# Bidirectional Mamba block with experts: both directions' outputs projected into one PSUM bank and added once a sequence

## The chip, the cores and the metric

The kernel runs on one core of a Trainium2 chip. It is one program whose five engines (TensorE, written PE in the profile; VectorE, DVE; ScalarE, ACT; GpSimd, POOL; SyncE, SP, which here only issues transfers) each work through a list of instructions in a fixed order and wait for one another by semaphores. The metric is the device time of one execution in microseconds (us), and less is better.

## The reference

The input x is 8 sequences of 512 tokens with 128 channels. It is normalised to xn, and the result is x plus an attention-like part of xn plus a mixture of experts of xn:

```
x   = x + attn(layernorm(x)) + ffn(layernorm(x))
attn: xn2 = layernorm(xn, g, b)
      out_f = mamba(xn2, f weights)
      out_b = reverse(mamba(reverse(xn2), b weights))
      attn  = concat(out_f, out_b) @ combine_w.T + combine_b + xn
mamba: xz = x @ in_w.T ; xi, z = split
      u = silu(conv4(xi)) ; dt, B, C = split(u @ x_w.T)
      delta = softplus(dt @ dt_w.T + dt_b)
      h[t] = h[t-1] * exp(delta*A) + delta*u * B[t]      (16 states)
      y = sum over states of h*C[t] + u*D ; return (y * silu(z)) @ out_w.T
ffn:  each token goes to the expert with the largest logit (8 experts):
      down(silu(gate(x)) * up(x))
```

A Mamba works on 256 inner channels with 16 states each. All numbers are float32. Both out_w and combine_w are linear, so the program multiplies them once at the start into one 256 x 128 matrix per direction, here called mo. The attention part of a sequence is therefore y_f times mo_f plus y_b times mo_b plus the bias combine_b.

## The kernel before

**Units and steps.** The work is cut into 16 units, one for each sequence and direction, in the order sequence 0 forward, sequence 0 backward, sequence 1 forward and so on. Units with an even number are forward passes, those with an odd number backward ones. A unit has 16 steps, one for each state, so the main loop of the program has 256 steps (and three more to empty the pipeline). In one step a state n of a unit is carried over all 512 tokens and both halves of 128 channels:

- `decay` (L764): ACT computes exp(delta*A) (L771) three steps ahead, and SP loads the row C of the state, spread over all partitions, from DRAM (`cs`, L778).
- `spread` (L792): PE brings delta\*u\*B into PSUM (tile `b`). For half of the states ACT has scaled it with B in `scaled` (L787), and PE only transposes it (L800). For the others PE spreads B over the partitions with a bfloat16 selector matrix (L805), and DVE multiplies it with delta\*u in `product` (L812).
- `scan` (L814): DVE runs the recurrence (L818), one instruction for each half.
- `times_c` (L835): POOL multiplies both halves of the state by C (L841). For a few states of the last unit C is brought into PSUM by a matmul in `spread_c` (L830) instead of by a transfer, and DVE multiplies (L839). [...]
- `sum_up` (L845): PE adds the product into the accumulator `py` in PSUM, three steps later (L855).

**What is woven in.** Everything else is put into the steps by hand. `plan` (L969) holds, for each step and each slot of a step ("ev", "ev2", "late", "pe0", "dv", "pe", "pe2"), what is to be issued there, and the loop at L1113 runs these slots in that order around the steps' own work. `prepare(v)` (L528) lists the preparation of unit v with its places in the steps of unit v-1: the norm, the input projection (`pi`), the convolution on DVE (L590), the gates (`pz`), the projection to dt, B and C (`px`), the step sizes (`pd`, L650), the softplus with a correction on POOL (`w`, L689 and L691 in `log1p` at step 9), and `delta` on DVE (L698) at steps 11 and 12, then delta times u on POOL (`du`, L709) and its transposes (`pdu`, L714). `conclude(v)` (L873) lists the end of unit v with its places in the steps of unit v+1: the gate (L881), the transposes back (`pyb`, L887 and L889) copied out by ACT (L906) at steps 4 and 5, the projection with mo (`po`, L914) in two halves at steps 7 and 8, and the addition to x by DVE (`total`, L929) at step 9. For a forward pass the bias is added to `po` by a float32 matmul of a row of ones with the bias (L921), one for each half of `po`. So an odd unit holds the projection of a forward pass, and an even one that of a backward pass. The last unit has an order of its own (`by_pairs`).

**The experts.** The tokens are ranked by expert in unit 1 and 2 (`arrange`). Then POOL scatters them with 32 indirect transfers to DRAM, sorted by expert (`scatter`, L408), one after the other from step 35 on, in units 2, 3 and 4 (L1007). From unit 4 on a group of four tiles of 128 sorted tokens is worked on in each unit: SP loads the tokens (`xe`, L434) and the weights (`we`, L422), PE runs the gate matmuls at steps 13 and 14 and the up matmuls of the group before in pieces at steps 3, 8 and 9 (`pg`, L457), DVE multiplies the two one step later each time (L481), and PE computes the way down at steps 10 and 11 (`pde`, L489). The results go back by indirect transfers (L500), are fetched at the end (`moe`) and added by POOL (L519).

**PSUM.** `py` has two of the eight banks, the tile `b` of `spread` rotates over four, and all other matmuls (`po`, `pg`, `pde`, `pd`, `pz`, `c` and so on) share two banks (`ps_mm`, L93). A matmul that takes one of these two waits until the tile that had it has been read.

```
ps_y, ps_b = pool("ps_y", 1, space=PS), pool("ps_b", 4, space=PS)
ps_mm = pool("ps_mm", 2, space=PS)
...
(7, "pe", do(project, range(2), False)),
(8, "pe", do(project, range(2, NJ), False)), (9, "dv", total),
...
for i in range(NT):
    add(o + 6 + i * 37 // NT, "ev", lambda i=i: scatter(i))
```

With o = 29 the last two lines put the scatters on the steps 35 to 70 without 42, 49, 57 and 64.

Of the kernel before, what the change touches and what calls it, by code (L numbers as in the profile page):

```python
# [32 lines left out]
F32 = mybir.dt.float32  # L33
BF16 = mybir.dt.bfloat16
# [5 lines left out]
P = 128  # L40
EPS = 1e-5
DIRS = ("f", "b")
L, D, DI, R, NS, KC, E = 512, 128, 256, 8, 16, 4, 8
NH, NJ = DI // P, L // P
# [6 lines left out]

ROWS, ROW_C, ROW_DT = 3 * NS, 64, 96
NX = ROW_DT + R


def columns():
# [20 lines left out]
def block_kernel(ctx: ExitStack, tc: tile.TileContext, a: dict, out: bass.AP):  # L77
    nc = tc.nc
    x = a["x"]
    NB = x.shape[0]  # L80
# [35 lines left out]

    rout = pk[:, at["rout"]]
    comb = halves("comb", D)
    comb_b = pk[0:1, at["comb_b"]]
    w = {}  # L120
    for i, d in enumerate(DIRS):
        w[d, "in"] = pk[:, at[d, "in"]]
# [65 lines left out]
    def selector():  # L188


        nothing = const.tile([P, 1], F32, name="nothing")
        nc.vector.memset(nothing, 0.0)
        for k in range(3):
            nc.gpsimd.affine_select(
                out=sel,
                in_=sel if k else nothing[:ROWS].unsqueeze(2).to_broadcast([ROWS, NS, P]), compare_op=ALU.not_equal, fill=1.0,
                base=-k * NS, pattern=[[-1, NS], [0, P]], channel_multiplier=1,
            )

    def project_weights(d, di):  # L200
        mo = const.tile([P, NH, D], F32, name=f"{d}_mo")
# [557 lines left out]
        return s % NS in sets.get(s // NS, BY_ACT)  # L759

    def c_in_psum(s):
        return s >= NSTEP - NS and s % NS in LAST_C

    def decay(s):  # L764

# [107 lines left out]
    def conclude(v):  # L873
# [20 lines left out]
        def block(y, h, j):  # L894
            return y[:, h, j, :] if len(y.shape) == 4 else y[:, h, j * P : (j + 1) * P]
# [6 lines left out]

        def back_end(h):
            if h == 0:
                c["y"] = tmp.tile([P, NH, L], F32, tag="y", name=f"y_{v}")
            nc.scalar.copy(c["y"][:, h, :], c["pyb", h])  # L906

        def project(js=range(NJ), whole=True):
            if whole or js[0] == 0:
                c["po"] = mm([P, NJ, D], f"po_{v}_{js[0]}")  # L910
            p = c["po"]
            for j in js:
                for h in range(NH):
                    nc.tensor.matmul(  # L914
                        p[:, j, :], block(c["y"], h, j), w[d, "mo"][:, h, :],
                        start=(h == 0 and (d == "b" or j == js[0])),
                        stop=(d == "b" and h == NH - 1), skip_group_check=(d == "f"),
                    )
            if d == "f":

                nc.tensor.matmul(  # L921
                    p[:, js[0] : js[-1] + 1, :], ones[0:1, :],
                    comb_b.unsqueeze(1).to_broadcast([1, len(js), D]),
                    start=False, stop=True, skip_group_check=True,
                )

        def total(js=range(NJ)):
            xs = xt[:, b * NJ + js[0] : b * NJ + js[-1] + 1, :]
# [1 line left out]

        def by_pairs():

            y = tmp.tile([P, NJ, NH, P], F32, tag="y", name=f"y_{v}")
            c["y"] = y.rearrange("p j h t -> p h j t")
            pairs = [range(k, k + 2) for k in range(0, NJ, 2)]
            for i, js in enumerate(pairs):
# [15 lines left out]
        if v == len(units) - 1:  # L952
# [3 lines left out]
            (2, "dv", gate),  # L956
            (3, "pe2", do(back, 0)), (4, "ev", do(back_end, 0)),
            (4, "pe2", do(back, 1)), (5, "ev", do(back_end, 1)),
            (7, "pe", do(project, range(2), False)),
            (8, "pe", do(project, range(2, NJ), False)), (9, "dv", total),  # L960
        ]

    def store(b):
        nc.sync.dma_start(
# [6 lines left out]
    def add(step, kind, f):  # L971
        plan[step, kind].append(f)
# [29 lines left out]
    for i, kind in (  # L1002
        (0, "dv"), (1, "ev"), (1, "dv"), (1, "pe2"), (2, "ev2"), (2, "dv"),
        (3, "dv"), (4, "ev"), (4, "dv"), (5, "ev"),
    ):
        add(o + i, kind, lambda: next(order_of, None))
    for i in range(NT):  # L1007
        add(o + 6 + i * 37 // NT, "ev", lambda i=i: scatter(i))

    begin = 4  # L1010
    groups = [list(range(k, min(k + GROUP, NK))) for k in range(0, NK, GROUP)]
# [37 lines left out]
        pass  # L1049
    weights("f")  # L1050
    selector()
    first.norm()
    first.turn()
    first.turn_end()
# [155 lines left out]
```

## Time and profile before

| | before |
|---|---|
| median of 3 runs | 952.93 us (952.07 to 959.26) |
| profiled execution | 953.34 us |
| its span, first to last instruction | 951.6 us |
| busy: PE, DVE, ACT, POOL | 850.2, 907.2, 803.0, 841.5 us |
| mean granted TensorE clock | 0.953 of full speed |
| `po` matmuls, forward and backward passes (L914) | 128 records each, 275 and 276 ns |
| bias matmuls (L921) | 32 records, 425 ns |
| additions to x (L929), 128 x 512 | 15, 677 ns |
| products with C on POOL (L841) and on DVE (L839) | 253 of 2362 ns; 6 of 679 ns |
| scatters (L409) | 32, 1015 ns |

The profile is one execution. A row of a group gives the line of the source, the engine, the operation, what it writes and reads with shapes, how often, and then the busy time in us with the mean of one in ns, and the idle time of the engine ahead of it with what ended it. A row of the timeline gives the start and the duration in us, the engine, the line and the operation, where neighbours of one kind are merged ("x8"), and in brackets the idle time ahead of it and what ended it. A float32 matmul is two records of the trace. Matmuls overlap one another, so a record's duration is longer than the distance to the next one.

### The profile page before, as it was taken

Reading aid. Unit: us, or ns where it says so; the run is one execution under the profiler, and the core shown is the slowest. Engines: PE = TensorE matmul, PEld = TensorE weight load, DVE = VectorE, ACT = ScalarE, POOL = GpSimd, SP = SyncE. Lnnn points to the kernel's source line nnn. Section 1 sums busy time; section 2 is a strip of 40 time slices with the busy share of each in tenths; the row PEclk is TensorE's granted clock in tenths of the full one; section 3 lists DMA queues with packets and bytes.
Section 4 is the critical chain, followed back from the end, with each engine's and each line's share of the span. In section 5 each row is a group of like instructions: output and inputs, shape, how many; then the busy total and the mean of one; then the engine's idle time right before and its main releaser. Section 6 shows DMA issues by size and latency. Waiting matters only on the chain.

```text
span 951.6 us, 16224 instructions
## 1 busy us (share of the span) xinstructions
PE 850.2 (89%) x5510; PEld 657.9 (69%) x5510; DVE 907.2 (95%) x1101; ACT 803.0 (84%) x1490; POOL 841.5 (88%) x524
## 2 busy tenths in 40 slices
PE   5699896978789889899998999989999999989897
PEld 2367574766567668777786877868777786767676
DVE  7999989999899999999999999999999999999996
ACT  5898986969679797998969989698988979799792
POOL 5689798799999979799897998979899898979995
PEclk9588999988979999999899999999999999999999
DMA  5364222222233625245441544425245341622262
GB/s 153 111 132 107 66 76 66 78 74 80 84 95 104 192 70 182 78 123 163 114 154 53 161 138 121 152 82 185 63 130 168 112 153 54 186 74 85 90 177 75
DMA packets 68483, 108.54 MB, mean 114 GB/s; under 512 B 6848, under 2 KB 29248, under 8 KB 68400
## 3 DMA queue, kind: packets, MB, share of 16 engines
q1 hardware_dynamic: 65552, 101.32, 36.0%
q0 software_dynamic: 2272, 4.67, 1.4%
q10 hardware_dynamic: 576, 1.51, 0.5%
q8 instruction: 44, 0.72, 0.3%
q14 instruction: 39, 0.32, 0.1%
HBM read 97.60 MB, written 9.87 MB: 113 GB/s over the span
## 4 chain that ended last, share of the span: by engine, by line
PE 42%; ACT 26%; DVE 18%; issue 7%; POOL 6%; DMA 1%; SPq 0%; POOLq 0%; DVEq 0%; ACTq 0%
PE py L855 14%; DVE hs L818 10%; ACT dA L771 8%; PE b L800 7%; ACT dbt L787 7%; PE pg L457 4%; PE pd L650 4%; POOL hs L841 3%; DVE b L812 3%; DVE acc L590 2%; PE pde L489 2%; PE po L914 2%; PE b L805 2%; ACT acc L582 1%; PE pdu L714 1%
## 5 line engine op out<-in xcount | busy, mean ns | idle before, releaser
L841 POOL TENSOR_TENSOR hs<-hs,cs 128x1024 f32<-128x1024 f32 x253 | 594.3, 2362 | 71.9 <-DVE hs L818 59.9
L818 DVE TENSOR_TENSOR_SCAN hs<-dA,b 128x512 f32<-128x512 f32 x512 | 592.8, 1206 | 0.1
L855 PE MATMUL py<-ident,hs 128*128 128x128 f32 x2048 | 279.3, 282 | 10.8 <-POOL hs L841 10.7
L855 PEld LDWEIGHTS py<-ident,hs 128*128 128x128 f32 x2048 | 234.4, 145 | 47.2 <-POOL hs L841 23.6
L787 ACT ACTIVATE dbt<-dut,bt 128x256 f32<-128x256 f32 x524 | 221.9, 496 | 0.1
L800 PE MATMUL b<-ident,dbt 128*128 128x128 f32 x1048 | 187.5, 289 | 19.6 <-DVE hs L818 10.4
L771 ACT ACTIVATE dA<-delta,b_A 128x512 f32<-128x512 f32 x256 | 168.2, 715 | 14.9 <-DVE hs L818 14.8
L800 PEld LDWEIGHTS b<-ident,dbt 128*128 128x128 f32 x1048 | 128.8, 145 | 74.1 <-ACT dbt L787 52.7
L771 ACT ACTIVATE dA<-delta,f_A 128x512 f32<-128x512 f32 x256 | 168.6, 715 | 8.3 <-DVE hs L818 6.3
L812 DVE TENSOR_TENSOR b<-du,b 128x512 f32<-128x512 f32 x250 | 159.8, 686 | 9.3 <-PE b L805 8.5
L599 PE MATMUL pz<-pk,xin 128*128 128x256 f32 x128 | 42.8, 492 | 29.3 <-DVE acc L590 25.4
L650 PE MATMUL pd<-cdt,pk 9*128 9x512 f32 x124 | 66.3, 635 | 0.0
L590 DVE SCALAR_TENSOR_TENSOR acc<-pi,pk,acc 128x511 f32<-128x511 f32 (+2 forms) x96 | 64.5, 739 | 0.1
L457 PE MATMUL pg<-xeT,we 128*128 128x128 f32 x468 | 61.8, 278 | 2.2 <-ACT z L610 2.1
L457 PEld LDWEIGHTS pg<-xeT,we 128*128 128x128 f32 x468 | 56.2, 192 | 5.5 <-ACT z L610 3.8
L599 PEld LDWEIGHTS pz<-pk,xin 128*128 128x128 f32 x128 | 30.2, 247 | 41.1 <-ACT dbt L787 26.5
L805 PE MATMUL b<-cdt,sel 48*128 48x512 bf16 x125 | 50.6, 405 | 8.6 <-DVE hs L818 8.6
L721 ACT COPY dut<-pdu 128x512 f32<-128x512 f32 x32 | 18.6, 585 | 34.6 <-PE pdu L714 34.6
L500 POOL DMA_INDIRECT by_token<-ye,to x39 | 39.6, 1016 | 6.3 <-issue 3.1
L646 POOL TENSOR_TENSOR cdt<-cdt 32x512 f32<-32x512 f32 (+1 forms) x32 | 33.1, 1034 | 7.8 <-ACT cdt L632 7.7
L489 PEld LDWEIGHTS pde<-we,g 128*128 128x128 f32 x234 | 27.6, 191 | 15.2 <-issue 7.6
L409 POOL DMA_INDIRECT sorted_in<-xn,row_i x32 | 32.5, 1015 | 5.3 <-issue 3.8
(170 smaller groups left out, 1054.8 us busy)
## 6 DMA issues: line engine op xcount, KB each, us to landing
cs<-cd SPq DMA_DIRECT2D x253, 256.0 KB, 3.5
we<-in_expert_w SPq DMA_DIRECT2D x39, 576.0 KB, 4.6
sorted_in<-empty SPq DMA_DIRECT2D x9, 258.0 KB, 7.9
xe<-sorted_in SPq DMA_DIRECT2D x9, 258.0 KB, 4.5
xt<-in_x SPq DMA_DIRECT2D x8, 256.0 KB, 7.3
moe<-by_token SPq DMA_DIRECT2D x8, 256.0 KB, 3.0
out<-xt SPq DMA_DIRECT2D x7, 256.0 KB, 3.7
pk<-in_pack ACTq DMA_DIRECT2D x1, 704.0 KB, 7.9
```

The costliest lines, as they stand in the source:

```text
L457: nc.tensor.matmul(p[:, q - 4 * b, :], T[ks[i]][:, which, c, :], G[ks[0], "xT"][:, i, :], start=True, stop=True,)
L590: nc.vector.scalar_tensor_tensor(c["acc"][:, h, k:], c["pi", h][:, : L - k], cw[:, h, KC - 1 - k : KC - k], c["acc"][:, h, k:], ALU.mult, ...
L599: nc.tensor.matmul(p[:, j, :], c["xin"][:, t : t + P], w[d, "in"][:, DI:], start=True, stop=True,)
L650: nc.tensor.matmul(p, w[d, "dt"][:, h * P : (h + 1) * P], cdt[ROW_DT : NX + 1], start=True, stop=True,)
L771: nc.scalar.activation(k["dA"][:, h, :], c["delta"][:, h, :], AF.Exp, scale=w[d, "A"][:, h, n : n + 1],)
L787: nc.scalar.activation(k["dbt"][:, j, :], c["dut"][:, j, :], AF.Copy, scale=c["bt"][:, j, n : n + 1],)
L800: nc.tensor.transpose(k["b", h][:, j * P : (j + 1) * P], k["dbt"][:, j, h * P : (h + 1) * P], ident,)
L805: nc.tensor.matmul(k["b", 0], sel[:, n, :], c["bc"], start=True, stop=True)
L812: nc.vector.tensor_mul(k["b", h], c["du"][:, h, :], k["b", 0])
L818: nc.vector.tensor_tensor_scan(k["hs"][:, h, :], k["dA"][:, h, :], k["b", h], 0.0, ALU.mult, ALU.add)
L841: nc.gpsimd.tensor_mul(k["hs"], k["hs"], k["cs"].unsqueeze(1).to_broadcast([P, NH, L]))
L855: nc.tensor.matmul(c["py"][:, j, h * P : (h + 1) * P], block[:, h, j * P : (j + 1) * P], weight, skip_group_check=True, **kw,)
```

## The change

There are three edits and a new timetable.

1. For sequences 0 to 6 the forward pass is no longer projected by itself. Its y is kept (the tile moves from a pool of one buffer to one of two), and when the backward pass of the sequence is concluded, PE projects both into one `po`: for each of the four token blocks two matmuls with mo_f and two with mo_b, at steps 7 and 8 as before. DVE adds the sum to x once. `total` moves from step 9 to step 10, for all units that have it. Sequence 7 keeps its two projections.
2. The bias is brought into `po` first, by one bfloat16 matmul over all 512 columns with a contraction of three rows. Three rows of the packed weights hold the bias, and `bias_pieces` (two subtractions on POOL at the start) leaves in them three pieces whose bfloat16 upper halves add up to the float32 value. The stationary operand is three rows of ones in bfloat16.
3. For state 6 of unit 3, C comes by a matmul into PSUM, and DVE multiplies, as for three states of the last unit; the load of C and the product on POOL go.
4. The scatters are put on the steps 35 to 71 without 40, 48, 52, 55 and 66.

In the order of the built program nothing else moves: ACT's list is the same, POOL's has the three new instructions at the start, one product less, and some scatters before or behind other neighbours.

```diff
--- before.py
+++ after.py
@@ -51,6 +51,9 @@
 
 ROWS, ROW_C, ROW_DT = 3 * NS, 64, 96
 NX = ROW_DT + R
+
+
+SCATTER, SCATTER_C = 3, (6,)
 
 
 def columns():
@@ -116,7 +119,10 @@
 
     rout = pk[:, at["rout"]]
     comb = halves("comb", D)
-    comb_b = pk[0:1, at["comb_b"]]
+    comb_b = pk[0:3, at["comb_b"]]
+    bias = comb_b.bitcast(BF16).rearrange("p (n two) -> p n two", two=2)[:, :, 1]
+    one_row = const.tile([3, P], BF16, name="one_row")
+    nc.gpsimd.memset(one_row, 1.0)
     w = {}
     for i, d in enumerate(DIRS):
         w[d, "in"] = pk[:, at[d, "in"]]
@@ -196,6 +202,12 @@
                 in_=sel if k else nothing[:ROWS].unsqueeze(2).to_broadcast([ROWS, NS, P]), compare_op=ALU.not_equal, fill=1.0,
                 base=-k * NS, pattern=[[-1, NS], [0, P]], channel_multiplier=1,
             )
+
+    def bias_pieces():
+
+
+        for m in (2, 1):
+            nc.gpsimd.tensor_sub(comb_b[:m], comb_b[:m], bias[:m])
 
     def project_weights(d, di):
         mo = const.tile([P, NH, D], F32, name=f"{d}_mo")
@@ -759,7 +771,7 @@
         return s % NS in sets.get(s // NS, BY_ACT)
 
     def c_in_psum(s):
-        return s >= NSTEP - NS and s % NS in LAST_C
+        return s % NS in {SCATTER: SCATTER_C, len(units) - 1: LAST_C}.get(s // NS, ())
 
     def decay(s):
 
@@ -902,27 +914,33 @@
 
         def back_end(h):
             if h == 0:
-                c["y"] = tmp.tile([P, NH, L], F32, tag="y", name=f"y_{v}")
+                c["y"] = two.tile([P, NH, L], F32, tag="y", name=f"y_{v}")
             nc.scalar.copy(c["y"][:, h, :], c["pyb", h])
 
         def project(js=range(NJ), whole=True):
-            if whole or js[0] == 0:
+
+            both_dirs = b < NB - 1
+            new = whole or js[0] == 0
+            if new:
                 c["po"] = mm([P, NJ, D], f"po_{v}_{js[0]}")
             p = c["po"]
+            biased = both_dirs or d == "f"
+            if new and biased:
+
+                nc.tensor.matmul(
+                    p, one_row, bias.unsqueeze(1).to_broadcast([3, NJ, D]),
+                    start=True, stop=False, skip_group_check=True,
+                )
+            terms = [(c["y"], w[d, "mo"])]
+            if both_dirs:
+                terms.insert(0, (C[v - 1]["y"], w["f", "mo"]))
+            terms = [(y, m, h) for y, m in terms for h in range(NH)]
             for j in js:
-                for h in range(NH):
+                for i, (y, m, h) in enumerate(terms):
                     nc.tensor.matmul(
-                        p[:, j, :], block(c["y"], h, j), w[d, "mo"][:, h, :],
-                        start=(h == 0 and (d == "b" or j == js[0])),
-                        stop=(d == "b" and h == NH - 1), skip_group_check=(d == "f"),
+                        p[:, j, :], block(y, h, j), m[:, h, :], start=not biased and i == 0,
+                        stop=i == len(terms) - 1, skip_group_check=biased,
                     )
-            if d == "f":
-
-                nc.tensor.matmul(
-                    p[:, js[0] : js[-1] + 1, :], ones[0:1, :],
-                    comb_b.unsqueeze(1).to_broadcast([1, len(js), D]),
-                    start=False, stop=True, skip_group_check=True,
-                )
 
         def total(js=range(NJ)):
             xs = xt[:, b * NJ + js[0] : b * NJ + js[-1] + 1, :]
@@ -930,7 +948,7 @@
 
         def by_pairs():
 
-            y = tmp.tile([P, NJ, NH, P], F32, tag="y", name=f"y_{v}")
+            y = two.tile([P, NJ, NH, P], F32, tag="y", name=f"y_{v}")
             c["y"] = y.rearrange("p j h t -> p h j t")
             pairs = [range(k, k + 2) for k in range(0, NJ, 2)]
             for i, js in enumerate(pairs):
@@ -956,9 +974,10 @@
             (2, "dv", gate),
             (3, "pe2", do(back, 0)), (4, "ev", do(back_end, 0)),
             (4, "pe2", do(back, 1)), (5, "ev", do(back_end, 1)),
+        ] + ([] if d == "f" and b < NB - 1 else [
             (7, "pe", do(project, range(2), False)),
-            (8, "pe", do(project, range(2, NJ), False)), (9, "dv", total),
-        ]
+            (8, "pe", do(project, range(2, NJ), False)), (10, "dv", total),
+        ])
 
     def store(b):
         nc.sync.dma_start(
@@ -1004,8 +1023,10 @@
         (3, "dv"), (4, "ev"), (4, "dv"), (5, "ev"),
     ):
         add(o + i, kind, lambda: next(order_of, None))
+
+    dates = [s for s in range(o + 6, o + 6 + 37) if s not in (40, 48, 52, 55, 66)]
     for i in range(NT):
-        add(o + 6 + i * 37 // NT, "ev", lambda i=i: scatter(i))
+        add(dates[i], "ev", lambda i=i: scatter(i))
 
     begin = 4
     groups = [list(range(k, min(k + GROUP, NK))) for k in range(0, NK, GROUP)]
@@ -1049,6 +1070,7 @@
         pass
     weights("f")
     selector()
+    bias_pieces()
     first.norm()
     first.turn()
     first.turn_end()
@@ -1178,7 +1200,7 @@
         c = slice(at["dt"].start + i * DI, at["dt"].start + (i + 1) * DI)
         pack[ROW_DT:NX, c] = v["dt_w"].T
         pack[NX, c] = v["dt_b"]
-    pack[0, at["comb_b"]] = inputs[pre + "combine_b"]
+    pack[:3, at["comb_b"]] = inputs[pre + "combine_b"]
     src["pack"] = pack
 
 
```

## The prediction

> **What bounds it.** I read the page's engine rows first, then the groups, then the waits of DVE and POOL, then the timeline of the stretches that the change touches.
>
> ```profile
> PE 850.2 (89%) x5510; PEld 657.9 (69%) x5510; DVE 907.2 (95%) x1101; ACT 803.0 (84%) x1490; POOL 841.5 (88%) x524
> ...
> L841 POOL TENSOR_TENSOR hs<-hs,cs 128x1024 f32<-128x1024 f32 x253 | 594.3, 2362 | 71.9 <-DVE hs L818 59.9
> L818 DVE TENSOR_TENSOR_SCAN hs<-dA,b 128x512 f32<-128x512 f32 x512 | 592.8, 1206 | 0.1
> ```
>
> DVE is idle for only 44 of 951.6 us: over the span it is the bound. But four engines are above 80%, so the question at each place is who is late there. DVE's own waits answer it:
>
> ```profile
> 196.97 0.70 DVE L698 SCALAR_TENSOR_TENSOR pd<-pd,w 128x512 f32<-128x512 f32 x1 [1.85 <-POOL w L691]
> 257.56 0.70 DVE L698 SCALAR_TENSOR_TENSOR pd<-pd,w 128x512 f32<-128x512 f32 x1 [4.02 <-POOL w L689]
> ...
> 439.29 1.29 DVE L812 TENSOR_TENSOR b<-du,b 128x512 f32<-128x512 f32 x2 [0.93 <-PE b L805]
> 475.54 1.29 DVE L812 TENSOR_TENSOR b<-du,b 128x512 f32<-128x512 f32 x2 [0.39 <-PE b L805]
> 478.31 0.69 DVE L929 TENSOR_TENSOR xt<-po,xt 128x512 f32<-128x512 f32 x1 [0.35 <-PE po L921]
> 479.40 0.69 DVE L481 TENSOR_TENSOR g<-g,pg 128x512 f32<-128x512 f32 x1 [0.40 <-PE pg L457]
> ```
>
> The reader is to see two regimes. In the scatter stretch (171 to 314 us) DVE waits for POOL, which the timeline shows with no wait for data from 171 to 329. Elsewhere DVE waits a few tenths for PE, above all in steps 7 to 9 of a unit, where po is computed. POOL waits for DVE early in every later unit (for 3.66 us at 855.64, the last time); after that it runs without a data wait to its last product at 941, so what DVE loses or gains after 856 doesn't reach the end.
>
> **The steps.** An odd unit carries the projection of a forward pass, an even one that of a backward pass. Costs below are distances from one start to the next in the timeline: scan 1.13, a 128x512 add 0.58, a half po (8 records) 0.9 to 1.0.
>
> (1) Odd units (1, 3, ... 13) lose po and the add. PE: 2 x (1.0 + 0.65 for the float32 bias of 256 columns) = 3.3 to 3.5 us less. DVE: the 0.58 add goes, and with it waits on a late PE. Unit 1: 0.58 + 0.35 (po) + 0.33 (b) + 1.06 (pd) = 2.3, taken as 2.0, since ranking the tokens follows. Unit 5: 0.58 + 0.17 = 0.75. Unit 7: 0.58 + 0.39 + 0.35 + 0.40 + 0.24 = 1.96. Units 9, 11, 13: 0.58 + 0.38 + 0.24 = 1.2 each. What is late next: at step 12 PE transposes du, which POOL writes (L709, ended 493.66 in unit 7). From there 0.5 for pdu, 1.0 for pg and 0.33 + 0.43 for b lie ahead of the product of state 16, which started at 497.11: no earlier than 495.9, a gain of 1.2. So unit 7 is capped at 1.2. Sum without unit 3: 2.0 + 0.75 + 4 x 1.2 = **-7.6**.
>
> (2) The scatter stretch. Of state 6 in unit 3 POOL loses its 2.36 us product; DVE gets two of L839 (679 ns, 1.2 to 1.4 us). Two scatters, 1.18 apart with their gap, move from before step 57 to after it, one from before step 41. At 257.56 POOL is then 2.36 + 2 x 1.18 = 4.7 us earlier and DVE's 4.02 wait nearly gone. But the scatters come back: by step 75 (313.96, where DVE waits 0.18 for POOL again) POOL has saved only the product. So the stretch, unit 3's add with it, gains **-2.4** and not 4.7. Ends: 0 (the product's slot filled by some other wait) and 4.7. The new matmul c (three took 3.4 us, 1.13 each) lies in a unit where PE is 82% busy; it holds a PSUM bank until DVE is through, and pd of step 6 may wait for it: 0 to 0.6, taken as 0. SP loses one 256 KB load. The last scatter goes from step 70 to 71, and SP's load of xe (306.14) waits for it; xe is read at 321.1, and the cs loads behind it in SP's queue have buffers of six: hidden, about 2 us if not.
>
> Here a rule speaks against the change. The Trainium skill (Perfetto Trace Analysis, Optimizing Scalar/DVE Operations) says that GpSimd and DVE share an SBUF port which a two-port DVE operation locks, so that moving work between them might not help. By it the stretch would gain nothing and pay 1.3. The row: L841 took 2338 to 2392 ns in a stretch where DVE worked beside it all the time, so POOL isn't being held up, and the product is worth its whole 2.36. I go with the row.
>
> (3) Even units. The doubled po costs PE 0.33 (bf16 bias, priced by L805, the same 512 columns) + 1.0 at step 7 and 0.9 at step 8: +2.3. Behind it stand b of the next states and the expert's pg, and DVE waits for those. The slack, in unit 10:
>
> ```profile
> 643.52 1.06 PE L914 MATMUL po<-b_mo,y 128*128 128x128 f32 x8
> 643.71 1.21 DVE L678 SCALAR_TENSOR_TENSOR w<-q,one 128x1024 f32<-128x1024 f32 x1
> 644.51 0.40 PE L805 MATMUL b<-cdt,sel 48*128 48x512 bf16 x1
> 645.95 1.28 DVE L812 TENSOR_TENSOR b<-du,b 128x512 f32<-128x512 f32 x2
> 645.99 1.06 PE L914 MATMUL po<-b_mo,y 128*128 128x128 f32 x8
> 646.88 1.06 PE L457 MATMUL pg<-xeT,we 128*128 128x128 f32 x8
> ...
> 648.26 0.67 DVE L929 TENSOR_TENSOR xt<-po,xt 128x512 f32<-128x512 f32 x1
> 648.84 0.69 DVE L481 TENSOR_TENSOR g<-g,pg 128x512 f32<-128x512 f32 x1
> ```
>
> b starts at 645.73 instead of 644.51, is done 0.43 later, and L812 is late by 0.21. po's second half runs 647.21 to 649.01, then pg to 650.11. The add is now a step later, so L481 is next in DVE at 648.47: it waits 1.64. Together 1.85 us; replayed to step 14 (b at 662.0 for 660.3) it stays 1.8. The add's later place costs nothing itself: the next pg waits for L481, not for the add. Part comes back: at state 16 DVE waits 0.93 for a b held up by POOL's du (the row at 439.29; 0.92 and 0.87 in units 10 and 12). So 1.8 - 0.9 = 0.9 in units 6, 10, 12. In unit 8 PE is already 0.91 late, so 0.21 becomes 0.73, and nothing comes back: 2.4. In unit 14 about 1.5, hidden behind POOL. Units 2 and 4 have no pg there and run in POOL's stretch: 0. Sum 3 x 0.9 + 2.4 = **+5.1**, between 1 (all absorbed) and 9 (nothing back, unit 14 visible).
>
> Another rule weighs against (1) and (3): the Trainium skill (TensorE: Matmul & The Clock Gate, What's actually happening) says PE falls to half clock after an idle window of about 3.4 us. Thinned odd units could then run a window of PE's steps at half speed, 1.7 us each, +10 over six units. The row: from 616 to 632 PE was busy 6.6 and 5.9 of each 8 us and the granted clock stayed 1.00; an odd unit without po is thinned no further than that. By the row 0.
>
> (4) Nothing: the bias pieces (two POOL subtractions, each under L646's 1.03) and the memset lie in POOL's 7.68 us wait before L646 at 22.08; uncovered about 2 us. y in two buffers frees no recorded wait. In the last unit the bias saves PE 0.9 and moves the add; POOL's chain sets that end: 0.
>
> **Sum:** -7.6 - 2.4 + 5.1 = -4.9. The profiled execution took 953.34 (span 951.6), 0.4 above the median of the runs shown; from the median 952.93 the same -4.9 gives **948.0**.
>
> **Rivals.** *Better than summed* (0.20): the cap on unit 7 doesn't hold, the stretch keeps 4.7, the 0.46 waits at state 18 of units 7 to 13 go, and the even units absorb their delay but for unit 8's 0.9: -2.3 - 4.7 - 0.75 - 2.4 - 3 x 1.66 + 0.9 = -14.2, 939. For it: PE runs without a gap through these steps, so 3.4 us is much relief. Against: POOL's du chain. *Only the instructions go* (0.16): waits are replaced by others; six adds of 0.58 and the POOL product save 5.9 and the even units take 5.1: 952. This is also the case that the change doesn't do what it says: the adds go but DVE idles in their place. *The doubled po becomes PE's bound* (0.14), which ends slower: with a half clock window in steps 7 to 9 of the even units (0.57 was granted from 528 to 532), the added 2.3 becomes 4.6 and DVE loses 1.8 + 2.3 = 4.1 in each of units 6, 8, 10, 12, of which 0.9 comes back in three: 16.4 - 2.7 - 10.0 = +3.7, 956.6. It decides from 2.5 us net lost per unit on (10.0 / 4). Against: the clock was 1.00 there in three of these four units.
>
> **Numbers.** Forecast 0.50, 948.0. A measurement of this kernel can tell about 1% from no change: below 943.4 or above 962.5. Faster by over 1% is most of the first rival and a tail of the forecast, 0.20; slower by over 1% is the part of the last rival where it goes further than worked out, 0.06; the rest 0.74. The range 939 to 957 holds the forecast's bounds, the second rival, and half of the other two.
>
> **To see after.** Right: no L929 in odd units, eight 128x512 adds in all for fifteen; the wait at the first delta of unit 3's step 11 gone or under 1 us, a new one of about 2 us for POOL's w at step 11 of unit 4; DVE waiting 1 to 2 us for pg in units 6 to 14. Wrong: pg waits of 3 us and more, a clock below 0.9 in steps 7 to 9 of even units, or no POOL wait left in unit 4 (the stretch gained more).

## The result and the profile after

The changed kernel took 956.62 us in the median of 20 runs (953.88 to 965.48), the kernel before, timed beside it, 952.9: ratio 1.0043 with a 95% interval of 1.0028 to 1.0059, that is +4.1 us (2.7 to 5.6). The forecast was 948.0, so the time went the other way. Executions over 1.5% above the fastest of the same kernel are left out of every median, ratio and mean clock below. The profiled execution of the changed kernel took 959.61 (span 957.9, granted clock 0.938), 3 us above its median; what is read from it below is read unit by unit and held against other executions.

The page's engine row and first groups, then four rows of the groups by form (busy us, mean ns, idle time ahead):

```profile
PE 857.1 (89%) x5488; PEld 666.0 (70%) x5488; DVE 903.8 (94%) x1096; ACT 804.0 (84%) x1490; POOL 840.7 (88%) x526
...
L853 POOL TENSOR_TENSOR hs<-hs,cs 128x1024 f32<-128x1024 f32 x252 | 592.4, 2363 | 79.3 <-DVE hs L830 56.8
L830 DVE TENSOR_TENSOR_SCAN hs<-dA,b 128x512 f32<-128x512 f32 x512 | 592.3, 1204 | 0.1
```

```profile
L940 PE MATMUL po<-f_mo,y 128*128 128x128 f32 x128 | 20.0, 281 | 0.0
L947 DVE TENSOR_TENSOR xt<-po,xt 128x512 f32<-128x512 f32 x8 | 5.3, 666 | 0.0
L851 DVE TENSOR_TENSOR hs<-hs,c 128x512 f32<-128x512 f32 x8 | 5.1, 680 | 4.3 <-PE c L842 4.3
L930 PE MATMUL po<-pk,one_row 3*128 3x512 bf16 x8 | 3.2, 398 | 0.0
```

The change did what it says: eight 128x512 adds for fifteen, one POOL product less, and a bias matmul of 0.40 us a record, like the matmul of L805 that it was priced by. DVE is busy 3.4 us less and yet ends later, so it waits more.

### The profile page after: what moved, and what is told of

Same layout as the page of the kernel before. It is cut to its first block, busy times and chain, and to the rows that moved or that the text cites. A ratio compares the mean times of both kernels' runs of the same rounds, so it can differ in the third digit from the quotient of the medians.

```text
span 957.9 us, 16171 instructions
## 1 busy us (share of the span) xinstructions
PE 857.1 (89%) x5488; PEld 666.0 (70%) x5488; DVE 903.8 (94%) x1096; ACT 804.0 (84%) x1490; POOL 840.7 (88%) x526
## 3 DMA queue, kind: packets, MB, share of 16 engines
q10 hardware_dynamic: 576, 1.51, 0.5%
## 4 chain that ended last, share of the span: by engine, by line
PE 46%; ACT 28%; DVE 15%; issue 5%; POOL 4%; DMA 1%; SPq 0%; POOLq 0%; ACTq 0%; DVEq 0%
PE py L867 15%; ACT dA L783 10%; ACT dbt L799 7%; DVE hs L830 7%; PE b L812 7%; PE pg L469 4%; PE pd L662 4%; PE pde L501 3%; DVE b L824 3%; POOL hs L853 2%; DVE acc L602 2%; PE po L940 2%; PE b L817 2%; PE pz L611 2%; PE pyb L901 1%
## 5 line engine op out<-in xcount | busy, mean ns | idle before, releaser
L867 PE MATMUL py<-ident,hs 128*128 128x128 f32 x2048 | 285.3, 286 | 11.9 <-POOL hs L853 11.7
L867 PEld LDWEIGHTS py<-ident,hs 128*128 128x128 f32 x2048 | 240.0, 147 | 45.1 <-issue 22.2
L812 PE MATMUL b<-ident,dbt 128*128 128x128 f32 x1048 | 190.0, 294 | 25.0 <-DVE hs L830 13.6
L812 PEld LDWEIGHTS b<-ident,dbt 128*128 128x128 f32 x1048 | 132.7, 149 | 78.4 <-ACT dbt L799 55.5
L611 PE MATMUL pz<-pk,xin 128*128 128x256 f32 x128 | 45.3, 515 | 28.3 <-DVE acc L602 24.8
```

The source lines that it names most:

```text
L611: nc.tensor.matmul(p[:, j, :], c["xin"][:, t : t + P], w[d, "in"][:, DI:], start=True, stop=True,)
L812: nc.tensor.transpose(k["b", h][:, j * P : (j + 1) * P], k["dbt"][:, j, h * P : (h + 1) * P], ident,)
L867: nc.tensor.matmul(c["py"][:, j, h * P : (h + 1) * P], block[:, h, j * P : (j + 1) * P], weight, skip_group_check=True, **kw,)
```

## Where the time went, unit by unit

A unit's length here is the distance from its first scan to the next unit's in the timeline. Setting all profiles side by side, the lengths of units 6 to 13 are not scattered: they take a few values, set by whether po is there and by whether a window of half clock (a stretch in which the granted clock is 0.50) lies on steps 7 to 8.5. There stand po, `one` (a matmul of one column, from which DVE forms w) and w. In each of the 19 traces the granted clock is either 1.00 or 0.50 and only changes at places a multiple of 3.41 us apart.

| unit | no half clock at steps 7 to 8.5 | half clock there |
|---|---|---|
| odd, forward po as before | 56.26, 56.25 (units 9 and 11 before) | 57.83 (unit 7 before) |
| odd, no po | 56.18, 56.16 (units 9 and 11 after) | 56.19, 56.14 (units 7 and 13 after) |
| even, po of one direction | 56.65 (unit 10 before) | 56.93 (unit 8 before) |
| even, doubled po | 57.71 (unit 8 after) | 59.28 (units 6, 10 and 12 after) |

So without a half clock window an odd unit gains 0.1, where 1.2 was predicted, and an even one pays 1.05, where 0.9 was predicted; with a window the odd one gains 1.6 and the even one pays 2.3. (Two windows in a row, at steps 7 to 9 of unit 13 of e3 below, made an odd unit without po 57.66 long.) A pair loses about 1.0 in the first case and 0.7 in the second. Unit 14 is hidden, as predicted: what it loses (1.15) unit 15 gives back. That holds without a window; with one on unit 14 (e16 below: 58.45) units 14 and 15 took 1.6 more than before. Unit 10 of the changed kernel (start, duration, engine, line; in brackets the idle time ahead and what ended it):

```profile
640.39 2.22 PE L662 MATMUL pd<-cdt,pk 9*128 9x512 f32 x4
...
643.46 1.91 PE L867 MATMUL py<-ident,hs 128*128 128x128 f32 x8
645.30 0.42 PE L697 MATMUL one<-ones 1*128 1x1 f32 x2
645.83 1.22 DVE L690 SCALAR_TENSOR_TENSOR w<-q,one 128x1024 f32<-128x1024 f32 x1 [1.00 <-PE one L697]
...
648.88 1.09 PE L867 MATMUL py<-ident,hs 128*128 128x128 f32 x8
648.99 1.30 DVE L824 TENSOR_TENSOR b<-du,b 128x512 f32<-128x512 f32 x2 [0.80 <-PE b L817]
...
652.91 0.69 DVE L493 TENSOR_TENSOR g<-g,pg 128x512 f32<-128x512 f32 x1 [1.51 <-PE pg L469]
```

The 1.51 for pg is the wait that was predicted (1.64). The eight py records at 643.46 take 1.91, those at 648.88 take 1.09: PE was at half clock ahead of po, `one` came 1.00 late and b 0.80. Of the scatter stretch, the first and last row are all of the waits for POOL that are left, and the two between are the longest of the others:

```profile
197.12 0.70 DVE L710 SCALAR_TENSOR_TENSOR pd<-pd,w 128x512 f32<-128x512 f32 x1 [0.25 <-POOL w L703]
...
225.07 1.29 DVE L893 TENSOR_TENSOR yt<-py,z 128x512 f32<-128x512 f32 x2 [1.59 <-PE py L867]
239.00 1.28 DVE L851 TENSOR_TENSOR hs<-hs,c 128x512 f32<-128x512 f32 x2 [1.35 <-PE c L842]
...
313.09 0.70 DVE L710 SCALAR_TENSOR_TENSOR pd<-pd,w 128x512 f32<-128x512 f32 x1 [0.46 <-POOL w L701]
```

The 4.02 at 257.56 are gone. In exchange DVE waits 1.35 for the new c, which the prediction left out, and 1.59 for py, where it waited 0.55 before.

## The experiments

The theory after the result: the scatter edits gain what was said, the odd units' relief is worth nothing, and the even units pay for the doubled po. The rival: windows of half clock make the loss, wherever po is.

| kernel | median us | ratio to before, 95% | mean clock of its runs |
|---|---|---|---|
| after | 956.62 | 1.0043 (1.0028 to 1.0059) | 0.949 |
| e1_scatter_only | 950.33 | 0.9967 (0.9952 to 0.9982) | 0.956 |
| e2_joint_only | 960.03 | 1.0055 (1.0031 to 1.0079) | 0.942 |
| e3_no_fwd_half | 949.94 | 0.9974 (0.9955 to 0.9994) | 0.944 |
| e4_po_behind_pg | 955.00 | 1.0005 (0.9987 to 1.0024) | 0.954 |
| e5_pd_128_rows | 955.38 | 1.0020 (0.9993 to 1.0047) | 0.954 |
| e6_du_first | 955.02 | 1.0003 (0.9980 to 1.0026) | 0.946 |
| e7_po_unread | 955.88 | 1.0018 (1.0004 to 1.0033) | 0.952 |
| e8_scatter_du_first | 949.25 | 0.9938 (0.9914 to 0.9962) | 0.956 |
| e9_pd_128_du_first | 952.90 | 1.0001 (0.9982 to 1.0020) | 0.952 |
| e10_best | 946.70 | 0.9933 (0.9913 to 0.9954) | 0.963 |
| e11_no_fwd_po | 947.92 | 0.9945 (0.9925 to 0.9966) | 0.950 |
| e12_split_late | 957.87 | 1.0066 (1.0041 to 1.0091) | 0.949 |
| e13_seq0_apart | 961.08 | 1.0086 (1.0055 to 1.0116) | 0.942 |
| e14_seq3to6_joint | 958.13 | 1.0047 (1.0028 to 1.0066) | 0.943 |
| e15_scatter_again | 950.30 | 0.9966 (0.9950 to 0.9981) | 0.955 |
| e16_after_again | 956.61 | 1.0047 (1.0025 to 1.0069) | 0.946 |
| e17_before_again | 954.05 | 1.0005 (0.9989 to 1.0021) | 0.953 |

Each ratio is to executions of the kernel before that were timed side by side with it; these had a mean clock of 0.950 to 0.952. The kernels were timed in groups: after; e1 to e4; e5 to e8; e9 to e12; e13 to e15; e16 and e17. Differences between kernels of different groups carry some 2 us of uncertainty, an estimate from the widths of the intervals. Within the changed kernel's 20 runs, 0.01 of mean clock goes with 3.3 us of time (correlation -0.75).

### The parts: e1, e15, e2, e3

e1 and e15 are the kernel before with `SCATTER, SCATTER_C`, `c_in_psum` and `dates` of the diff; e2 is the changed kernel without them. e3 leaves the forward terms out of the joint po:

```diff
-            if both_dirs:
-                terms.insert(0, (C[v - 1]["y"], w["f", "mo"]))
```

> The kernel before with only the C of state 6 of unit 3 by PSUM and the new scatter dates. Theory (the scatter stretch gains as summed, the loss lies in the even units): about 950.9, that is -2.0 against before, with DVE's waits for POOL between 171 and 314 us down from 5.9 to about 1 us. Rival (the stretch's waits are only replaced by others): within 0.5 of before, 952.9. Rival (POOL and DVE hamper each other): slower than before by up to 1.3.

> The changed kernel with C of state 6 of unit 3 and the scatter dates as before, so only the joint projection, the bias in pieces and the add at step 10. Theory (the joint projection is the whole loss, the stretch pays back 2): about 958.6, that is +5.7 against before. The steps as predicted would give -2.5 (950.4). If the stretch's edits were the loss: about 952.

> The changed kernel leaving out the forward half of the joint projection (16 of the 32 records of po in each even unit; the outputs lack that part), so that an even unit's PE has the work it had before plus the bf16 bias, and an odd unit none. Theory (the doubled po in the even units is the loss, odd units give nothing): the pg waits of 1.5 us in units 6 to 14 shrink to about 0.4, and the time falls by 4 times 1.9 to about 949. By the prediction's sum it would fall to 943 (the -7.6 of the odd units would then stand alone). Rival (half clock windows, whatever the length of po, make the loss): stays within 1 of 956.6, with granted clocks below 0.92 again in steps 5 to 7 of the even units.

> The kernel before with the C of state 6 of unit 3 by PSUM and the new scatter dates once more, as the base of the other two: about 950.3, 0.997 of the kernel before.

The scatter edits gain 3.1 and, again, 3.2 us: the step was right and a little small. The joint projection alone costs 5.2. e3 splits it: against e1 it only has the relief of the odd units (with the bias pieces, y's second buffer and the add's later place), and it is not faster, 0.9974 against 0.9967. Its runs had a mean clock of 0.944 for 0.956, so half clock has a part in this; but in its profile unit 11 takes 56.16, 0.1 less than in e1, and with windows units 7, 9 and 13 take 56.81, 56.88 and 57.66. Putting the forward half back (after against e3) costs 0.0069, 6.6 us. The odd units' -7.6 are therefore the step that is missing, and the even units' +5.1 came out at 6.6.

### po behind pg: e4

```diff
-            (8, "pe", do(project, range(2, NJ), False)), (10, "dv", total),
+            (8, "pe3", do(project, range(2, NJ), False)), (10, "dv", total),
```

with a slot "pe3" run after "pe2".

> The changed kernel with the second half of po issued behind the expert's up matmuls (pg) of step 8 instead of ahead of them. Theory (DVE's wait for pg is most of the loss of an even unit): the waits of 1.5 us for pg go in units 6 to 14, up to 1.5 in each of units 6, 8, 10 and 12, part of which comes back as a wait for b or for the next pg one step later: 951 to 954. Rival (half clock windows ahead of po make the loss): the pg waits go, but the time stays within 1 of 956.6.

The wait for pg at step 8's end goes, and comes back a step later as 0.97 for the next pg, and as 0.24 for pd (unit 10, at 650.54 and 657.72). Units 6, 10 and 12 take 57.70, 57.70 and 57.71, what a doubled po takes without a half clock window in the other order. It is PE's amount of work between steps 7 and 10 that costs 1.05, not its order. This profile has one half clock window at steps 7 to 8.5 (unit 8) for five in the changed kernel's. The kernel gains 1.6 by the medians and 3.6 by the ratios, where 2.6 to 5.6 were expected; the mean clock of 0.954 for 0.949 would make 1.7 of that, an estimate at the 3.3 us for 0.01 above.

### POOL's chain: e6 and e8

```diff
-            times_c(s)
+            if s % NS == 12 and s // NS in (7, 9, 11, 13):
+                held.append(s)
+            else:
+                times_c(s)
```

where the held product is issued after the next step's "ev" slot, so that both du stand together on POOL. e8 does it in units 6 to 14 of e1.

> The changed kernel with POOL's second delta-times-u product (du, step 13) issued ahead of the C product of step 12 in units 7, 9, 11 and 13, not behind it. Theory (the relief of the odd units is lost because POOL's chain du, pdu, dut, b sets the product of state 16): the waits of 0.5 to 1.0 us for b at state 16 of these four units go, and with du 2.36 us earlier the relief is had: about 2.9 less, 953.7. Rival (something else caps these units, or the C product of step 12, then 1.3 us later, becomes what is waited for): within 1 of 956.6.

> The kernel before with the C of state 6 of unit 3 by PSUM and the new scatter dates, and POOL's second delta-times-u product ahead of the C product of step 12 in units 6 to 14. Theory (POOL's du chain sets state 16): the waits of 0.9 us for b at state 16 of units 6, 10 and 12 go and odd units gain a few tenths: 3 less than the 950.3 of the same kernel without the new order, about 947.5. Rival (another chain is as late): 950.3 within 1.

How the odd units lose their relief is in unit 9, first before, then after (POOL's second du, PE's b, DVE's product of state 16):

```profile
606.92 1.27 POOL L709 TENSOR_TENSOR du<-delta,u 128x512 f32<-128x512 f32 x1
609.82 0.40 PE L805 MATMUL b<-cdt,sel 48*128 48x512 bf16 x1
610.31 1.29 DVE L812 TENSOR_TENSOR b<-du,b 128x512 f32<-128x512 f32 x2
```

```profile
608.06 1.26 POOL L721 TENSOR_TENSOR du<-delta,u 128x512 f32<-128x512 f32 x1
610.85 0.40 PE L817 MATMUL b<-cdt,sel 48*128 48x512 bf16 x1
611.34 1.29 DVE L824 TENSOR_TENSOR b<-du,b 128x512 f32<-128x512 f32 x2 [1.00 <-PE b L817]
```

From du's start to the product it is 3.39 us before and 3.28 after: before, too, DVE got there just as b was ready, so whatever DVE gains ahead of it turns into the wait of 1.00. In e6 du comes earlier and the wait shrinks:

```profile
599.44 2.50 POOL L721 TENSOR_TENSOR du<-delta,u 128x512 f32<-128x512 f32 x2
...
605.57 0.69 DVE L824 TENSOR_TENSOR b<-du,b 128x512 f32<-128x512 f32 x1 [0.31 <-PE b L817]
```

Unit 9 falls to 55.47, unit 7 to 55.48, 0.7 less each; by the ratios the kernel gains 3.8 us, by the medians 1.6, on either side of the 2.9 expected. In e8 units 6 and 10 fall by 0.7 (55.92 and 55.93), so the chain binds there too when po is single. Its odd units, for which a few tenths were expected, gain nothing (56.28 and 56.27 in units 7 and 11), and against e1 the kernel gains 2.8 us by the ratios and 1.1 by the medians for an expected 3.

### Is PE's relief worth anything: e7

The forward projection's 32 records stay in the odd units, into a PSUM tile that is not read.

```diff
-        ] + ([] if d == "f" and b < NB - 1 else [
+        ] + ([(7, "pe", do(fill, range(2))), (8, "pe", do(fill, range(2, NJ)))]
+             if d == "f" and b < NB - 1 else [
```

> The changed kernel with the forward projection's 32 records of po kept in the odd units 1 to 13 into a PSUM tile that nobody reads, with no bias and no add: PE gets about 2 us of work back in each odd unit. Theory (PE's relief in the odd units is worth nothing): within 1 of 956.6 from units 3 to 13, and faster by up to 2 if PE's relief lets unit 1 fall to half clock (there 17 us of half clock for 0 before). The prediction's steps, in which PE's relief is most of -7.6: slower by about 4 (960.5).

With its work given back to PE, the kernel is no slower (955.88 for 956.62), and units 9, 11 and 13 lie at 56.20, 56.40 and 56.19. PE's relief, 4.1 of the -7.6 (the rest is six adds of 0.58), is worth nothing there. The mean clock rises a little, 0.952 for 0.949.

### Half clock at steps 7 to 8.5: e5, e12, e9

The matmul pd of step 6 multiplies 9 rows. e5 runs it over all 128, where the other 119 meet zero weights, and moves the first `split` (on POOL) from step 6 to step 8; e12 moves only the split; e9 is e5 with du first in units 6 to 14.

```diff
-            (6, "pe", do(steps_of, 0)), (6, "pe", do(steps_of, 1)),
+            (6, "pe", do(steps_of, 0, "dt_all", slice(0, P))),
+            (6, "pe", do(steps_of, 1, "dt_all", slice(0, P))),
...
-            (6, "ev", do(split, 0)), (9, "ev2", do(split, 1)),
+            (8, "ev", do(split, 0)), (9, "ev2", do(split, 1)),
```

> The changed kernel with the step-size matmul of step 6 (pd) contracted over 128 rows, of which all but 9 meet zero weights, in place of 9; the first split on POOL goes from step 6 to step 8. Same number and length of matmuls. Theory (a half clock window falls on steps 7 and 8 whenever the two pd matmuls, which use 9 of 128 rows, fill the window before it, and it costs an even unit 1.5 us more): the half clock windows at steps 6 to 9 go, the mean clock rises from 0.949 to about 0.955, and the time falls by 2 to 4: about 953.5. Rival (rows don't matter to the clock): 956.6 within 1, clock unchanged.

> The changed kernel with only POOL's first split moved from step 6 to step 8 (pd with 9 rows as before): a control for the kernel with 128 rows. Theory (the rows, not the split, took the half clock windows away): 956.6 within 1, clock about 0.949, and half clock windows at steps 7 to 9 in two or more of units 6 to 14. Rival (the split was it): no such window.

> The changed kernel with both remedies: the pd matmuls of step 6 over 128 rows, and POOL's second delta-times-u product ahead of the C product of step 12 in units 6 to 14. Theory (two independent losses): the sum of what each brought alone (-1.2 and -1.6): about 953.8, no half clock window at steps 7 to 9 of units 6 to 14, units 7, 9, 11 and 13 at 0.7 under the kernel before's. Rival (they stand in for one another): 955.

Two views of stretches, the changed kernel and e9, each around the pd of unit 10 (stretch, its length, busy us and instructions of each engine, granted clock, DMA share, GB/s):

```profile
638.60:642.00 3.40, 3.40 (x19) 1.93 (x17) 3.40 (x5) 3.40 (x8) 3.40 (x3) 1.00 0.77 265
642.00:645.40 3.40, 3.40 (x14) 2.52 (x13) 2.84 (x3) 3.28 (x6) 3.40 (x2) 0.50 0.65 174
645.40:648.80 3.40, 3.40 (x24) 2.70 (x24) 2.35 (x2) 3.40 (x8) 3.40 (x3) 1.00 0.83 260
```

```profile
635.90:639.30 3.40, 3.40 (x19) 2.12 (x19) 3.40 (x5) 3.39 (x8) 3.40 (x2) 1.00 0.84 266
639.30:642.70 3.40, 3.40 (x27) 2.81 (x26) 3.40 (x4) 3.28 (x6) 3.34 (x3) 1.00 0.85 205
```

PE counts as busy for all 3.40 us of the first stretch, and is granted half clock in the next. With 128 rows it stays at 1.00. In the four profiles with 128 rows (e5, e9, e10, e11) not one of the units 5 to 14 has half clock at steps 7 to 8.5; the changed kernel's two profiles have five and four, the kernel before's two each, e3's, e7's and e14's four to five, e15's three, e4's one, and only e1's has none as well. The control e12 keeps the changed kernel's clock (0.949), is no faster, and its profile (an execution of 968.90 us) has such windows in four of these units, so it is the rows and not the split.

Laid on the 3.41 us grid, the 15 profiles with 9 rows have 113 windows in steps 4 to 7 of the units from 5 on in which PE was busy over nine tenths, at full clock, and pd took 0.4 of the time or more; 49 were followed by half clock. With 128 rows it was 0 of 28. What tells the 49 from the other 64 is not seen.

Units 6, 10 and 12 of e5 lie at 57.35 to 57.37 in place of 59.28. The time falls less than that, to 955.38; 1.2 (2.2 by the ratios) where 2 to 4 were expected. Part of it goes to half clock elsewhere: e5 and e9 have a window at steps 9 to 10 of units 5 and 11, which have no po (unit 11 takes 57.09 in both, unit 9 of e5 without a window 56.24), each behind one in which PE was busy 0.45 to 0.60 of the time. With du first as well (e9) it is 952.90, level with the kernel before, and 0.9 under what was expected.

### Half clock where po is missing: e10 and e11

e10 is e8 with the 128 rows, without a joint projection. e11 is e10 with the forward projections of sequences 0 to 6 and their adds left out:

```diff
-            (7, "pe", do(project, range(2), False)),
+        ] + ([] if d == "f" and b < NB - 1 else [
+            (7, "pe", do(project, range(2), False)),
```

> The kernel before with C of state 6 of unit 3 by PSUM, the new scatter dates, du ahead of the C product of step 12 in units 6 to 14, and pd of step 6 over 128 rows; no joint projection. Theory: 1 to 2 less than the 949.3 of the same kernel with 9 rows, since the half clock windows at steps 7 to 9 go: about 948. Rival (without the doubled po such a window costs nothing): 949.3.

> The kernel of e10_best leaving out the forward projections, their bias and their adds in units 1 to 13 (the outputs lack that part), with nothing put into the even units: the relief of the odd units alone, where POOL's du no longer stands ahead of state 16. The prediction's steps gave this relief 7.6 us. Theory (with POOL's cap moved by one product each odd unit gains 0.7 to 0.8, and units 1 and 5 little): 3 less than e10_best. If the relief is worth nothing whatever POOL does: no less than e10_best.

e10 at 946.70 (948 was expected) is the fastest kernel of this study, 6.4 us under the kernel before (4.4 to 8.3). Against e8 the 128 rows bring 2.5 by the medians and 0.5 by the ratios, which is within the uncertainty.

e9 and e10, timed side by side, differ in the joint projection alone (with its bias pieces, y's second buffer and the add's place), and neither has half clock at steps 7 to 8.5 of units 5 to 14. e9 takes 6.5 us more by the ratios. Its even units 6 to 12 take 57.36 or 57.37 for 56.00 to 56.02, and its odd units 7, 9 and 13 only gain 0.34 each. So the loss is there without half clock ahead of po: the rival named at the head of the experiments does not hold, and such a window only adds to the loss.

e11, with less to do than e10, is not faster: 1.2 slower by the medians of six executions each, within the intervals, where 3 less was expected. Its unit 13, then the same place in e10, where po is still computed:

```profile
808.40:811.80 3.40, 1.81 (x12) 1.18 (x10) 3.40 (x5) 3.40 (x8) 3.40 (x3) 1.00 0.61 230
811.80:815.20 3.40, 3.33 (x16) 3.21 (x16) 3.02 (x4) 3.40 (x8) 3.32 (x2) 0.50 0.24 80
```

```profile
809.00:812.40 3.40, 3.40 (x29) 3.07 (x29) 3.36 (x5) 3.40 (x8) 3.32 (x3) 1.00 0.25 92
812.40:815.80 3.40, 3.40 (x22) 2.29 (x20) 3.40 (x5) 2.75 (x6) 3.40 (x3) 1.00 0.03 7
```

And what e11 pays for it in that unit:

```profile
810.79 1.68 PE L805 MATMUL b<-ident,dbt 128*128 128x128 f32 x4 [1.44 <-ACT dbt L792]
...
816.34 0.69 DVE L485 TENSOR_TENSOR g<-g,pg 128x512 f32<-128x512 f32 x1 [1.52 <-PE pg L461]
```

Without po PE runs out of work at step 8, is busy 1.81 of 3.40 us, and the next 3.4 us are granted at 0.50. Units 11 and 13 take 57.16 and 56.68 instead of 55.92 and 55.81; unit 9, where no window falls, takes 55.53 for 55.92. So even with POOL's cap moved, an odd unit's relief is 0.4 at full clock and a loss of 0.9 to 1.2 where a window falls. The changed kernel's own two profiles have no window that begins at step 9 or 10 of units 5 to 14. Of the other kernels without a forward po there, e3, e4, e5 and e9 have some as well; in the seven profiles in which PE still has that work none occurs.

### Unit 1, and the sequences apart: e13, e14, e16, e17

e14 has `range(3, NB - 1)` where e13 has the following; e16 and e17 are the two kernels once more.

```diff
-            both_dirs = b < NB - 1
+            both_dirs = b in range(1, NB - 1)
...
-        ] + ([] if d == "f" and b < NB - 1 else [
+        ] + ([] if d == "f" and b in range(1, NB - 1) else [
```

> The changed kernel with sequence 0 projected as before (forward part, bias and add in unit 1, backward part alone in unit 2), sequences 1 to 6 jointly. Theory (unit 1 without a forward po falls to half clock and gains nothing): unit 1 within 0.3 of the kernel before's 60.8 with no half clock window, and 1 to 2.5 less than the changed kernel: about 954.5. The prediction's steps, by which unit 1 gains 2.0: slower by 2.0 (958.6).

> The changed kernel with only sequences 3 to 6 projected jointly (so units 8, 10, 12 and 14 doubled, 7, 9, 11 and 13 relieved), 0 to 2 as before. Theory (each doubled unit costs 1.05, or 2.6 with a half clock window on it, unit 14 is hidden, and the relieved ones give nothing): 3 to 5 more than the kernel with the scatter edits alone in the same call. The prediction's steps: 4.2 for units 8, 10 and 12 less 4.8 for the odd ones, 0.6 less than that kernel.

> The changed kernel once more. If the place of the half clock windows is a matter of how a free-running grid lies to an execution, and not of the program alone, units 6, 10 and 12 are again at either +1.05 (no window at steps 7 to 8.5) or +2.6 (one there) against the kernel before, but not the same units as in the first profile, and unit 1 may be anywhere from -2 to +3. Rival (the program fixes the windows): the same units as before, within 0.1. Time: 1.004 of the kernel before.

> The kernel before once more, beside the one above: units 9 to 14 within 0.1 of the first profile where no half clock window lies at steps 7 to 8.5, and a few tenths more where one does, since po is half as long; unit 1 at 60.8 without a half clock window and 3 to 5 us longer with 14 to 17 us of half clock, as with a forward po it was in e13 and e15.

The expectation for unit 1 was wrong. With its forward po back it took 65.57 in e13, with the same 17 us of half clock as in the changed kernel, where it took 63.03. First the changed kernel's waits there, then e13's:

```profile
117.81 1.29 DVE L824 TENSOR_TENSOR b<-du,b 128x512 f32<-128x512 f32 x2 [1.50 <-PE b L817]
124.89 1.22 DVE L690 SCALAR_TENSOR_TENSOR w<-q,one 128x1024 f32<-128x1024 f32 x1 [2.44 <-PE one L697]
```

```profile
118.76 1.29 DVE L824 TENSOR_TENSOR b<-du,b 128x512 f32<-128x512 f32 x2 [1.50 <-PE b L817]
125.80 1.22 DVE L690 SCALAR_TENSOR_TENSOR w<-q,one 128x1024 f32<-128x1024 f32 x1 [2.40 <-PE one L697]
129.85 1.29 DVE L824 TENSOR_TENSOR b<-du,b 128x512 f32<-128x512 f32 x2 [1.70 <-PE b L817]
137.10 1.29 DVE L824 TENSOR_TENSOR b<-du,b 128x512 f32<-128x512 f32 x2 [0.91 <-PE b L817]
```

The waits ahead of po are the same, the 1.70 behind it is gone without po. At an equal clock the missing po does gain 2.5, a little over the 2.0 that the prediction gave unit 1, and e13 as a whole is slower than the changed kernel. But the clock is not equal: the two profiles of the kernel before, and e1, e7 and e10, have no half clock in unit 1 at all (60.57 to 61.50), while none of the profiles without a forward po there is free of it. Half clock can fall on unit 1 with a po in it too (e8, e13, e14, e15), so this is a leaning, not a rule, and why unit 1 falls to half clock stays open.

e14 takes 7.8 us more than e15 by the medians, where 3 to 5 were expected. In the profiles units 8 to 13 give 4.2, as expected, and units 14 and 15 another 1.6, with a window on unit 14. Unit 1, which the edit doesn't touch, takes 68.91 against 64.04. Why such executions are more frequent in some kernels is open. e16 and e17 repeat the result, 1.0047 against 1.0005. e16 has the same few lengths at other units: 6 and 12 now at 57.70 and 57.71, unit 10 again at 59.28, unit 1 at 63.19. In e17 unit 6 has a window and takes 56.97. So which unit is hit belongs to the execution, what a hit costs belongs to the program.

## Why the prediction was wrong, point by point

- **Step (1), odd units, -7.6: this is the step that failed.** By e3 against e1 it is about +0.7, by e11 against e10 +1.2, both within their intervals of nothing. The cap by POOL's chain (du, its transposes, b) was seen, but worked out from unit 7 alone, whose half clock window (57.83) had made DVE late; there it left 1.2, and unit 7 did gain 1.6. In units 9 to 13 the product of state 16 stood at the cap already, and 0.1 was gained. Unit 1's -2.0 became +2.3, with 17 us of half clock in it for none before (in e16 6.8 us of it and +2.4). The waits of 0.38 and 0.24 for PE that were added up as gains were not what set these units' length.
- **The clock, taken as 0.** The Trainium skill (TensorE: Matmul & The Clock Gate, What's actually happening) has PE fall to half clock after an idle window, and the prediction set a row against it in which PE was busy 5.9 of 8 us. That row was a mean over more than two windows. e11 shows more than the rule says: a window that was not idle, with 1.81 busy of 3.40, was followed by 0.50, and it cost its relieved unit more than the relief. The other half clock, ahead of po, follows windows in which PE was busy throughout, and the page's rule does not foretell it; the last rival placed a window there and gave it 14%. The 1.00 read there in three of four units belonged to one execution. The sign of being wrong that was named for it, a clock below 0.9 in steps 7 to 9 of even units, was seen in units 6, 10 and 12.
- **Step (2), -2.4: right**, measured -3.1 and -3.2. The wait of about 2 us expected in unit 4 is 0.46, so the stretch kept more than the one product; the new c, for which no wait was counted, cost DVE 1.35. The port that the prediction weighed against it cost nothing that can be seen.
- **Step (3), +5.1: the mechanism right, the size short by the clock.** Without a window 1.05 a unit for 0.9, the pg wait 1.51 for 1.64, the product's wait 0.33 for 0.21, the 0.9 at state 16 recovered, unit 14 hidden. A half clock window adds 1.6. The 2.4 of unit 8 was read from a profile with a window there. With a window in both kernels an even unit does pay 2.3; unit 8 itself paid 0.8, since the changed kernel's profile had no window on it. Measured 6.6 in all, inside the 1 to 9 that were given.
- **Step (4)**: the bias pieces, y's buffer and the last unit were not tried by themselves; they lie within e3 against e1.

Of the rivals, the one in which the doubled po becomes PE's bound came nearest, at 956.6, and that was luck: its sum kept the odd units' gain of 7.6, which was not there, and charged 16.4 - 2.7 = 13.7 for the even ones, which cost 6.6. The runs give -3.1 + 0.7 + 6.6 = 4.2 (e1, then e3 against it, then after against e3). Each of these starts where the one ahead ends, so they divide the measured +4.1 and are no check of it.

## What to carry to other kernels

Ahead of a gain by relief on one engine, look in each place, not in one unit for all, at what releases the next common point; where the other chain arrives at the same time, the relief is worth nothing (a gain of 0.1 where 1.2 was predicted). Moving work from one stretch to a fuller one could cost twice here: the full stretch paid (1.05 a unit), and the thinned one sometimes fell to half clock (0.9 to 1.2 a window in e11). The scatter edits with a shorter binding chain (du first) and full rows in pd brought 946.7 where the scatter edits with the joint projection brought 956.6. And one profile does not tell where half clock falls: the next execution of the same kernel had it in other units.

## What the runs showed of the hardware

- A TensorE that is busy for a whole 3.4 us window can still be granted half clock in the next: 3.40 of 3.40, then 0.50, with pd over 9 rows. This followed 49 of 113 such windows in 15 profiles. Over 128 rows, at the same number of matmuls, it followed none of 28 in four profiles. How activity is counted is not seen.
- A half clock window at steps 7 to 8.5 costs a unit 0.0 us without po (56.19 for 56.18), 0.3 with a single po in an even unit (56.93 for 56.65), 1.6 with one in an odd unit (57.83 for 56.25) and 1.6 with a doubled one (59.28 for 57.71).
